# The shifted queries of a second attention layer: one VectorE subtraction from PSUM becomes a ScalarE copy and a GpSimd subtraction

## The chip, the core and the metric

The kernel runs on one core of a Trainium2 chip. The metric is the time of one execution on the device, in microseconds (us). Profile lines come from one further execution that the hardware profiler recorded; times in them count from the start of its span. PE is TensorE's matmul, PEld its weight load, DVE is VectorE, ACT is ScalarE, POOL is GpSimd and SP is SyncE. L12 is line 12 of the kernel.

## The reference

The program is a two-layer block of four batches of 512 tokens, 256 wide, in fp32. Each layer adds a gated cross-attention (16 heads of 16) and a gated feed-forward to the running x, each on a layer norm of x. Cut to what matters here:

```python
# layer 0: attention with biases and a decay over |t - s|, then a feed-forward with ternary weights
# layer 1:
def _L1_xattn_ref(q, k, v, Wq, Wk, Wv):
    qp = jax.nn.relu(jnp.einsum('bnd,od->bno', q, Wq))
    kp = jax.nn.relu(jnp.einsum('bnd,od->bno', k, Wk))
    vp = jax.nn.relu(jnp.einsum('bnd,od->bno', v, Wv))
    ...                                  # split into 16 heads
    E = NORM * jnp.einsum('bqhd,bkhd->bhqk', qh, kh)
    A = jax.nn.softmax(E, axis=-1)
    out = jnp.einsum('bhqk,bkhd->bqhd', A, vh)
    return out.reshape(B, N, -1)

x = x + tanh(g_xattn[0]) * _L0_xattn_ref(_layernorm(x), ctx, ctx, ...)
x = x + tanh(g_ffn[0])   * _L0_ffn_ref(_layernorm(x), ...)
x = x + tanh(g_xattn[1]) * _L1_xattn_ref(_layernorm(x), ctx, ctx, ...)
x = x + tanh(g_ffn[1])   * _L1_ffn_ref(_layernorm(x), ...)   # one of four experts for each token
```

The softmax needs each query row's largest score subtracted ahead of the exponential.

## The kernel before

**Groups and units.** The attention of both layers is cut into 32 groups, numbered in order of layer, batch, half of the features (tt) and parity of the head (e): groups 0 to 15 are layer 0, 16 to 31 layer 1, four to each batch. A group has four heads, each in 32 rows of the 128 partitions. Every group has four units, one for each 128 keys or queries, so there are 128 units; the unit u belongs to group u // 4.

**The score passes.** `scores(u, ...)` runs two kinds of score in quads. `maxima` makes scores of 128 queries against all keys for the unit six ahead (tiles pm), and VectorE reduces each 128 x 512 bank to a column of row maxima (L512). `weights` makes scores of 128 keys against all the *shifted* queries of unit u (tiles psc), and ScalarE takes the exponential of each bank (L527). A quad is two pm banks and two psc banks: that many matmuls run beside each other, since each uses 32 rows of the array. All PSUM tiles come from one ring of eight banks, so a bank that is drained late holds up the matmul that is eight allocations behind.

**The shift.** Row maxima come out with queries in the partitions, but queries stand with features in the partitions. `shifted(s)` turns the maxima tile m by four PE transposes into one bank pmT (L569), and VectorE subtracts it from the group's queries, q2 = q - pmT (L571). A spare row of each head's 32 carries the maximum, so the subtraction puts the shift into the operand of the second score pass.

**After the scores.** `weighted(s)` multiplies the exponentials with the values (L555, tile po), and ScalarE copies the result out (L561). `divided(s)` turns it by four transposes (tile pn), and VectorE takes reciprocals (L609), multiplies them with the gate in layer 1 (L611) and multiplies the weighted values with them (L616, tile o). In layer 1 it then adds o to x (L623): on GpSimd, but on VectorE for the last group of batches 2 and 3.

**The order.** Every engine executes in the order in which the program issues. After the scores of a unit, `slot(u)` issues what else belongs there. At the second of each group's units this is

```python
if u % NT == 2 and u > 0:
    s = u // NT
    if s + 1 < len(groups):
        shifted(s + 1)
        used += 0.5
    if s > 0 and not by_blocks(s - 1):
        divided(s - 1)
        used += 0.5
```

so shifted(s + 1) stands ahead of divided(s - 1), and one whole unit of scores lies between it and the first use of its q2. Behind these two, a small planner fills the slot from chains of jobs with costs and due times: layer norms (DVE statistics, POOL and ACT), projections of keys, queries and values (L455, L467, L469, L489, L491, L437, L439), the first layer's feed-forward (L668, L676, L383), the routing of tokens to experts (L755 to L772) and the dispatch lists (L816 to L1014), and the first expert tiles (L1037 and L1053 fetch rows and weights by POOL, L1090 multiplies, L1095 copies out). After the attention the remaining expert tiles follow in a hand-written queue, from about 700 us to the end.

**Tiles by tag.** A pool gives tiles with the same tag the same place. The tag "wo0" has one place of 128 x 512 fp32; it holds the first layer's output weights, which `residual` (L383) reads last for batch 3 of layer 0.

Of the kernel before, what the change touches and what calls it, by code (L numbers as in the profile page):

```python
# [11 lines left out]
F32 = mybir.dt.float32  # L12
U32 = mybir.dt.uint32
AF = mybir.ActivationFunctionType
ALU = mybir.AluOpType
# [4 lines left out]
P = 128  # L20
B, S, D = 4, 512, 256
# [30 lines left out]
def flamingo_kernel(ctx: ExitStack, tc: tile.TileContext, t: dict, out: bass.AP):  # L52
    nc = tc.nc
# [4 lines left out]
    const = ctx.enter_context(tc.tile_pool(name="const", bufs=1))  # L58
# [5 lines left out]
    def bank_psum(name):  # L64
        return ps.tile([P, 512], F32, tag="bank", name=name)
# [37 lines left out]
    wo0 = const.tile([P, NC, D], F32, tag="wo0", name="wo0")  # L103
# [288 lines left out]
    xTs, qs, ks, q2s, pos, os_ = {}, {}, {}, {}, {}, {}  # L392
# [170 lines left out]
    def shifted(s):  # L563

        g = groups[s]
        m = m_sb[g[0]][g[3]]
        pm = bank_psum(f"pmT{s}")
        for n in range(NT):
            nc.tensor.transpose(pm[:, ts(n, P)], m[:, n].rearrange("p h w -> p (h w)"), ident)  # L569
        q2s[g] = act.tile([P, S], F32, tag="q2", name=f"q2_{s}")  # L570
        nc.vector.tensor_tensor(q2s[g], qs[g], pm, ALU.subtract)  # L571

# [624 lines left out]
    def slot(u):  # L1199
# [4 lines left out]
# [8 lines that stand above are left out]
# [38 lines left out]
    for u in range(-NT, n_units):  # L1250
        if u == 0:
            shifted(0)
            early_values()
            other_constants()
        if u == 4:
            maxima_places(1)
        if u == first_unit(0, B - 1) + 1:
            attn_w.append(load_attn(1))
        if u == first_unit(1, 2) + 2:

            wo1 = [const.tile([P, NF // 2, D], F32, tag=f"cT{i}", name=f"wo1{i}") for i in range(2)]
            for i, w in enumerate(wo1):
                rw = t["wo1"][i * FF // 2 : (i + 1) * FF // 2, :]
                nc.sync.dma_start(out=w, in_=rw.rearrange("(c p) f -> p c f", p=P))
        vs = [u + NT] if u < 0 else [2 * u + NT, 2 * u + NT + 1] if u < LEAD - NT else [u + LEAD]
        scores(u, [v for v in vs if v < n_units])
        if u < -NT + 2:
            values[u + NT][0]()
        if u == -NT + 1:
            early_rows()  # L1270
        if u == -1:
            keys[0](halves=[1])
        if u in totals:
            job, i = totals[u]
            job(i)
        slot(u)
# [193 lines left out]
```

## Time and profile before

| What | us |
|---|---|
| median of 3 runs | 847.55 (846.2 to 848.15) |
| the profiled execution | 847.92 |
| its span | 845.8 |
| PE busy | 811.0 (96%) |
| DVE busy | 569.1 (67%) |
| ACT busy | 422.2 (50%) |
| POOL busy | 270.9 (32%) |
| DVE L571, 32 in all | 21.6 |

The span is the time from the first to the last instruction of the profiled execution. Busy shares are averages over the whole span; PE's busy time includes matmuls that wait within the array, and the ends of matmuls are modelled. In the rows of groups, the numbers behind the bar are busy time and the mean length of one in ns, and behind the second bar the idle time of the engine ahead of them with what ended it. In the timeline a row has start, length, engine, line, operation and count, and in brackets the idle time ahead of it.

### The profile page before, as it was taken

The numbers are of one execution on the slowest core, as the hardware profiler recorded it, in microseconds if no ns is written. First come the engines' busy times: TensorE is split into PE (matmuls) and PEld (weight loads), VectorE is DVE, ScalarE is ACT, GpSimd is POOL, SyncE is SP. The second block draws the span as 40 slices with busy tenths as digits, with TensorE's granted clock in tenths as the row PEclk, the third lists the DMA queues.
The fourth block names the chain that finished last, engine by engine and source line by source line (L and its number), as shares of the span: only waits on it lengthen the run. The fifth ranks groups of instructions, "written<-read, shape, count | busy, mean of one in ns | idle before, by whom it ended". The sixth has DMA issues, their size and how long they took to land. (4 is left out here: it accounts for less than half of the span.)

```text
span 845.8 us, 13576 instructions
## 1 busy us (share of the span) xinstructions
PE 811.0 (96%) x5220; PEld 452.4 (53%) x5220; DVE 569.1 (67%) x1272; ACT 422.2 (50%) x884; POOL 270.9 (32%) x439
## 2 busy tenths in 40 slices
PE   6999999999999999999999999999999999898994
PEld 3444444535464345544474444554545557787993
DVE  6768868766857776568737676558688654786443
ACT  2475555653645453455426474346556667332341
POOL 5536445524333243321101120002103314526522
PEclk9999999999999999999999999999999999999997
DMA  8200000000001000000000010000104422707730
GB/s 314 68 1 1 1 1 1 2 1 1 1 1 38 1 1 1 1 26 1 1 1 26 1 46 6 1 1 1 51 2 150 144 96 89 255 13 243 258 138 19
DMA packets 17712, 42.27 MB, mean 50 GB/s; under 512 B 2033, under 2 KB 12017, under 8 KB 15217
## 3 DMA queue, kind: packets, MB, share of 16 engines
q0 software_dynamic: 5104, 27.34, 9.3%
q1 hardware_dynamic: 12128, 13.54, 4.7%
q8 instruction: 41, 0.67, 0.3%
q10 hardware_dynamic: 416, 0.54, 0.2%
q14 instruction: 23, 0.18, 0.1%
HBM read 35.13 MB, written 6.29 MB: 49 GB/s over the span
## 5 line engine op out<-in xcount | busy, mean ns | idle before, releaser
L512 DVE TENSOR_REDUCE m<-pm 128x1 f32<-128x512 f32 x512 | 316.7, 681 | 109.0 <-PE psc L498 106.5
L527 ACT ACTIVATE p<-psc 128x512 f32<-128x512 f32 x512 | 267.1, 602 | 151.8 <-PE psc L498 149.4
L498 PE MATMUL psc<-q,k 32*128 32x512 f32 x1024 | 278.7, 623 | 0.2 <-DVE h L676 0.2
L498 PE MATMUL pm<-k,q 32*128 32x512 f32 x1024 | 262.7, 616 | 1.5 <-ACT q L485 0.9
L530 POOL TENSOR_TENSOR p<-p,dec 128x256 f32<-128x256 f32 x128 | 93.7, 736 | 178.7 <-ACT p L527 178.7
L498 PEld LDWEIGHTS pm<-k,q 32*128 32x128 f32 x1024 | 92.9, 184 | 84.1 <-issue 50.2
L498 PEld LDWEIGHTS psc<-q,k 32*128 32x128 f32 x1024 | 106.3, 184 | 52.0 <-issue 25.9
L555 PE MATMUL po<-p,v 128*32 128x512 f32 x1024 | 116.5, 595 | 1.9 <-DVE m L512 1.9
L555 PEld LDWEIGHTS po<-p,v 128*32 128x32 f32 x1024 | 31.7, 109 | 81.8 <-issue 60.8
L1090 PE MATMUL pg<-xs,wg 128*128 128x128 f32 x608 | 71.6, 276 | 0.4 <-DVE m L512 0.4
L1090 PEld LDWEIGHTS pg<-xs,wg 128*128 128x128 f32 x608 | 69.8, 192 | 3.8 <-DVE m L512 1.4
L623 POOL TENSOR_TENSOR x<-x,o 128x256 f32<-128x256 f32 x14 | 10.2, 727 | 174.4 <-DVE o L616 131.7
L1116 ACT ACTIVATE ha<-pg,wg 128x128 f32<-128x128 f32 x120 | 34.2, 368 | 53.0 <-PE pg L1090 53.0
L668 PE MATMUL ph<-xTf,w1q 128*128 128x512 f32 x128 | 60.0, 605 | 0.0
L1285 PE MATMUL pyf<-wo,ha 128*128 128x256 f32 x256 | 59.3, 387 | 0.0
L383 PE MATMUL py_f<-w2q,h 128*128 128x256 f32 x256 | 57.2, 381 | 0.0
L561 ACT COPY oT<-po 128x512 f32<-128x512 f32 x32 | 18.7, 584 | 77.1 <-PE po L555 77.1
L383 PEld LDWEIGHTS py_f<-w2q,h 128*128 128x128 f32 x256 | 48.0, 190 | 9.3 <-DVE m L512 3.0
L1285 PEld LDWEIGHTS pyf<-wo,ha 128*128 128x128 f32 x256 | 48.7, 195 | 6.4
L455 PE MATMUL pk<-cT,wk 128*128 128x512 f32 x68 | 35.3, 644 | 7.2 <-DMA cT<-in_ctxT_dram 7.2
L668 PEld LDWEIGHTS ph<-xTf,w1q 128*128 128x128 f32 x128 | 22.6, 189 | 30.4 <-issue 18.2
L388 DVE SCALAR_TENSOR_TENSOR x<-py_f,tg,x 128x512 f32<-128x512 f32 x8 | 6.0, 751 | 42.8 <-PE py_f L383 42.8
(256 smaller groups left out, 816.5 us busy)
## 6 DMA issues: line engine op xcount, KB each, us to landing
x<-in_x_dram SPq DMA_DIRECT2D x4, 512.0 KB, 8.7
rows_d<-xn_f SPq DMA_DIRECT2D x4, 512.0 KB, 3.0
rows_d<-x SPq DMA_DIRECT2D x4, 512.0 KB, 3.4
cT<-in_ctxT_dram SPq DMA_DIRECT2D x3, 512.0 KB, 9.5
w1q<-in_w_dram SPq DMA_DIRECT2D x1, 1024.0 KB, 9.0
w2q<-in_w_dram SPq DMA_DIRECT2D x1, 1024.0 KB, 11.3
wo<-in_wo_dram SPq DMA_DIRECT2D x2, 512.0 KB, 3.8
rows<-in_rows_dram SPq DMA_DIRECT2D x1, 640.0 KB, 9.2
```

The costliest lines, as they stand in the source:

```text
L383: nc.tensor.matmul(py[:, n, :], lhsT=operand(c, n0 + n), rhs=w[:, c, :], start=(c == 0), stop=(c == chunks - 1),)
L455: nc.tensor.matmul(pp, lhsT=attn_w[layer][w][:, c, ts(tt, P)], rhs=src[:, c, :], start=(c == 0), stop=(c == NC - 1),)
L498: nc.tensor.matmul(out_, lhsT=lhs[r, ts(n, P)], rhs=rhs[r, :], start=True, stop=True)
L512: nc.vector.tensor_reduce(m[:, n, 2 * pair + i, r : r + 1], pm[i], AX.X, ALU.max)
L527: nc.scalar.activation(p[:, i, :], psc[i], AF.Exp, scale=SCALE)
L530: nc.gpsimd.tensor_tensor(d, d, dec.unsqueeze(1).to_broadcast([P, 2, P]), ALU.mult)
L555: nc.tensor.matmul(po[i * HP : (i + 1) * HP, :], lhsT=v_sb[b % 2][0][:, kt, c0 : c0 + HP], rhs=ps_exp[NT * s + kt, i // 2][:, i % 2, :], s ...
L561: nc.scalar.copy(pos[s], po)
L668: nc.tensor.matmul(ph, lhsT=w1q[:, c, ts(f, P)], rhs=st["xT"][:, c, :], start=(c == 0), stop=(c == NC - 1),)
L1090: nc.tensor.matmul(ph[:, f, :], lhsT=w[:, c, ts(f2 * NF // 2 + f, P)], rhs=xs[j][:, c, :], start=(c == 0), stop=(c == NC - 1),)
L1116: nc.scalar.activation(ha[:, f, :], (ha if src is None else src)[:, f, :], AF.Gelu, bias=biases[j][:, fa : fa + 1],)
L1285: nc.tensor.matmul(py, lhsT=hs[j, f // 4][:, f % 4, :], rhs=wo1[f // 4][:, f % 4, :], start=(f == 0), stop=(f == NF - 1),)
```

## The change

For the groups of layer 1 from batch 1 on (groups 20 to 31, twelve calls), `shifted` no longer lets VectorE subtract from PSUM. ScalarE copies the bank pmT into a tile in SBUF, whose place is that of wo0, and GpSimd subtracts this tile from the queries. The other twenty groups are as before, and so is the order in which things are issued.

```diff
@@ -568,7 +568,13 @@
         for n in range(NT):
             nc.tensor.transpose(pm[:, ts(n, P)], m[:, n].rearrange("p h w -> p (h w)"), ident)
         q2s[g] = act.tile([P, S], F32, tag="q2", name=f"q2_{s}")
-        nc.vector.tensor_tensor(q2s[g], qs[g], pm, ALU.subtract)
+        if g[0] == 1 and g[1] > 0:
+
+            turned = const.tile([P, S], F32, tag="wo0", name=f"mT{s}")
+            nc.scalar.copy(turned, pm)
+            nc.gpsimd.tensor_tensor(q2s[g], qs[g], turned, ALU.subtract)
+        else:
+            nc.vector.tensor_tensor(q2s[g], qs[g], pm, ALU.subtract)
```

## The prediction

> **What bounds the kernel now.** I read the page first, then the busy time by stage, then the rows of the instructions that the change touches, and last the timeline around each of the twelve places where it acts. The twelve lie between 456.6 and 684.3 us (layer 1, batches 1 to 3), so that stage is what counts.
>
> ```profile
> 455.00:700.00 245.00, 242.11 (x1669) 122.06 (x1666) 169.42 (x376) 137.20 (x266) 42.25 (x74) 1.00 0.13 45
> ```
>
> The columns are the window, its length, then busy time of PE, PEld, DVE, ACT and POOL, clock, DMA. TensorE has a matmul in flight for 242.1 of 245.0 us at full clock. VectorE is busy 69%, ScalarE 56%, GpSimd 17%. So there are only 2.9 us in which PE stands quite still, and time can be won only there and where PE runs one of its two score streams (pm, psc) alone because a PSUM bank is not free yet.
>
> ```profile
> L571 DVE TENSOR_TENSOR q<-q,pmT 128x512 f32<-128x512 f32 x32 | 21.6, 675 | 1.1 <-PE pmT L569 1.1
> ...
> L561 ACT COPY oT<-po 128x512 f32<-128x512 f32 x32 | 18.7, 584 | 77.1 <-PE po L555 77.1
> ...
> L623 POOL TENSOR_TENSOR x<-x,o 128x256 f32<-128x256 f32 x14 | 10.2, 727 | 174.4 <-DVE o L616 131.7 <-DVE top L755 31.9 <-DVE left_d L816 10.8
> ...
> L725 POOL TENSOR_TENSOR x<-x,rows 128x1024 f32<-128x1024 f32 x3 | 7.1, 2358 | 6.3 <-ACT xn_f L360 6.3
> ```
>
> The first row is what is removed twelve times. The second is the price of the new ScalarE copy (same shape, also from PSUM). The last two bracket the new GpSimd subtraction.
>
> Now one of the twelve places, group 25, in order of time (start, length, engine):
>
> ```profile
> 569.48 0.66 PE L569 MATMUL pmT<-ident,m 128*128 128x128 f32 x4
> ...
> 570.67 0.67 DVE L571 TENSOR_TENSOR q<-q,pmT 128x512 f32<-128x512 f32 x1
> ...
> 571.26 0.25 DVE L609 RECIPROCAL rec<-pn 128x16 f32<-128x16 f32 x1
> ...
> 571.80 2.31 ACT L527 ACTIVATE p<-psc 128x512 f32<-128x512 f32 x4 [1.10 <-PE psc L498]
> ...
> 571.81 0.42 DVE L616 TENSOR_TENSOR o<-pn,rec 128x256 f32<-128x256 f32 x1
> ...
> 572.31 0.73 POOL L623 TENSOR_TENSOR x<-x,o 128x256 f32<-128x256 f32 x1 [23.19 <-DVE o L616]
> ...
> 573.23 2.45 DVE L512 TENSOR_REDUCE m<-pm 128x1 f32<-128x512 f32 x4
> ...
> 573.95 0.30 PEld L498 LDWEIGHTS pm<-k,q 32*128 32x128 f32 x4 [1.30 <-DVE m L512]
> ...
> 577.39 3.64 PE L555 MATMUL po<-p,v 128*32 128x512 f32 x32 [0.52 <-DVE m L512]
> ```
>
> VectorE runs without a pause from L571 to the reductions, and twice PE waits for a reduction to free a bank. ScalarE stands idle 1.10 us just after the transposes, and GpSimd has been idle 23 us. Here the moved 0.675 us is on the path.
>
> **The change part by part.** Of 32 shifted() calls, 20 keep L571. For the other twelve:
>
> 1. *Removed from DVE*: each L571 holds DVE from its start to the next instruction's start, 0.60 us (570.67 to 571.26 above; starts overlap). I use 0.60, 12 x 0.60 = 7.2 us of DVE work.
>
> 2. *Added to ACT*: 12 x 0.584 = 7.0 us. From the timeline, the time between the last exponential before the transposes' end and ScalarE's next instruction is over 1 us at eleven of the twelve (group 25: 570.70 to 571.80; group 22: 498.60 to 500.15) and 0.55 us at group 30, where a small copy (lT, L747) slips by under 0.1 us with PE busy. What hides it is PE, which is still making the next scores; without that cover it would cost up to 7.0 us. The copy also frees pmT's bank, at most 0.4 us after the old subtraction's end (0.6 at group 31), and much earlier at group 28.
>
> 3. *Added to POOL*: between 728 ns for 256 elements and 2358 for 1024 a straight line gives 728 + 1630/3 = 1.27 us for 512, so 15.3 us on an engine that is idle 83%. It issues no DMA itself, but it stands ahead of L623 and of whatever that slot issues: L623 comes up to 1.0 us later, and at groups 30 and 31 so do a bias copy (L1080) and a row fetch (L1037, at 668.04 and 686.75). The trace names nobody who waited for L623, and the two fetches bring tiles 0 and 1 back for output_tile, which runs after the attention: zero, with over 10 us of cover. SP's queue is not touched.
>
> 4. *The longer way to q2*: the copy starts when ACT's last exponential ends, takes 0.58, POOL starts 0.14 us after ACT (median of 54 such hand-overs from L527 to L530), 1.27 more: about 2.0 us. Before, it was DVE's backlog plus 0.67. The first score that reads q2 comes 3.2 us or more after the old subtraction's end at eleven groups and 2.27 us after it at group 28 (632.39 to 634.67). The new way ends 0.8 to 2.0 us later than the old one, but at group 28 about 0.9 us *earlier* (ACT is free at 629.47, DVE only at 631.72). Priced at zero, cover at least 1.8 us (group 25); each us beyond that would be lost whole, PE having nothing else to do. The single turned buffer is rewritten four units (some 20 us) later, and its place (wo0) was last read by layer 0: also zero.
>
> 5. *What DVE's 0.60 us is worth*, place by place:
>  - group 25: two PE waits on L512, as shown. -0.60.
>  - group 28: the second score quad's psc starts at 633.34, right after L616 frees pn's bank at 633.29. -0.50, less than the whole because an earlier pm of that quad is limited otherwise.
>  - groups 23 and 27: a score waits for DVE's L676 (PE stands 0.18 us, PEld 1.01) and L439 (PEld 0.67). In both, DVE's route chain sits before it, see below. -0.40 and -0.50.
>  - group 21: PE's next job waits 0.11 us beyond the usual 0.76. -0.10.
>  - groups 20, 22, 26: DVE idles 0.5 to 0.7 us a little later, waiting for ScalarE's half of the same bank (L437, L467), which waits for PE. 0.
>  - groups 24, 30, 31: DVE idles 2.4 to 5.3 us right behind, or PE is busy with output products. 0.
>  - group 29: next paragraph. +0.50.
>
> **The port.** The row that speaks against the change is this, at group 27 (and likewise at 521.52, and L820 at 685.28, 0.79 us):
>
> ```profile
> 611.16 0.73 POOL L623 TENSOR_TENSOR x<-x,o 128x256 f32<-128x256 f32 x1 [15.96 <-DVE top L755]
> ...
> 611.41 0.52 DVE L758 TENSOR_TENSOR onehot<-onehot,order 128x16 f32<-128x16 f32 x1
> ```
>
> and the group of that instruction (minimum, median, maximum in ns):
>
> ```profile
> L758 DVE TENSOR_TENSOR onehot<-onehot,order x4: 174/345/515, 521.5 to 732.9; 128x16 f32<-128x16 f32 x4
> ```
>
> L758 takes 174 ns alone and 515 ns when a GpSimd tensor_tensor runs; it ends 0.03 us after that does. [...] At groups 23 and 27, L758 would now arrive at about 520.9 and 610.75 and be let in when the subtraction ends (521.4, 611.35), still 0.5 to 0.6 us before its old end; hence the gains above. At group 29, the last addition of batch 2 runs on DVE with two SBUF inputs (L623, 648.29 to 648.71). It would arrive at 647.65, meet a subtraction of 647.6 to 648.9 and end at 649.25: 0.5 us late, with bn_stats and four reductions queued behind it, and PE's L1090 waiting for the first of those already. Hence +0.50.
>
> [...]
>
> Sum: -0.60 - 0.50 - 0.40 - 0.50 - 0.10 + 0.50 = -1.6 us. The profiled execution took 847.92 us (span 845.8 and 2.1 around it), so its counterpart is 846.3; the median of the runs is 847.55, 0.37 lower, which makes 845.9. The tail after 700 us begins with work handed down from this stage, so I carry the shift through unchanged.
>
> **The rivals.**
> - *DVE limits more than the gaps show* (0.17). VectorE's four reductions need 2.4 us of a bare unit of 2.5 us, and PE's modelled ends hide waits. If nine of twelve places pass on the whole 0.60, the gain is 5.4 - 0.5 = about 4.9 us: 842.6. Against it: the 2.9 us of standing PE in the stage.
> - *PE is the bound and gives nothing* (0.13). Each early release is met by a later wait for PE or ACT (DVE idles on psc 39.5 us in this stage). 847.5.
> [...]
> - *The edit acts late*, with q2 waited for by PE: needs 1.8 us and more beyond the worked-out way; I fold it into the slower case.
>
> **How the numbers follow.** The likeliest case has 0.45: its own range is -3.0 to 0, centred on 1.6, and about 0.2% (1.7 us) is also what a measurement of this kernel can tell from no change, so it splits into 0.25 faster and 0.20 same. Faster: 0.25 + 0.17 = 0.42; same: 0.20 + 0.13 = 0.33; slower: 0.25. The range 843.2 to 849.6 leaves out most of the strong gain's upper half and the port's full price, together about 0.2.
>
> **What would show it.** L571 x20; twelve L561-like copies of about 0.58 us from PSUM; POOL subtractions of 1.2 to 1.35 us; L611 at 234 ns in all (right) or above 1 us in some (the port); DVE's L623 at group 29 stretched from 424 ns to over 1 us; the 1.30 us wait at group 25 back near 0.7; no PE wait that names POOL's q2. A PE wait on q2, ACT's exponentials starting later behind the copy, or subtractions over 2 us would make the prediction wrong.

## The result, and the profile after

| | before | after |
|---|---|---|
| median of 18 runs (us) | 846.92 | 845.87 |
| range (us) | 846.16 to 848.25 | 844.03 to 846.76 |
| profiled execution, span (us) | 847.92, 845.8 | 846.76, 845.1 |

The ratio is 0.9982, 95% interval 0.9975 to 0.9989: 1.5 us less by the ratio, between 0.9 and 2.1. By the medians it is 1.05 us, because this before, over 18 runs, lies 0.6 us under the three runs that the forecast started from. The forecast was -1.65 us, which lies within this interval.

The stage of the change, in the same window as before (PE, PEld, DVE, ACT, POOL, clock, DMA):

```profile
455.00:700.00 245.00, 242.07 (x1684) 123.15 (x1678) 167.35 (x366) 144.34 (x281) 58.30 (x86) 1.00 0.13 45
```

VectorE is busy 2.1 us less, ScalarE 7.1 us more, GpSimd 16.1 us more, and PE is as busy as before. VectorE should have lost 7.2 us by the removed instructions alone. Some 3 us of that came back as instructions that were held, most of it in the L617 row and the last row of the groups below. The work also runs earlier by then, so that the last 2 us of the window hold 0.7 us that lay behind it before. The rest, over 1 us, is not accounted for.

```profile
L575 POOL TENSOR_TENSOR q<-q,mT 128x512 f32<-128x512 f32 x12 | 15.3, 1272 | 131.3 <-ACT mT L574 131.3
L577 DVE TENSOR_TENSOR q<-q,pmT 128x512 f32<-128x512 f32 x20 | 13.5, 676 | 0.0
...
L629 POOL TENSOR_TENSOR x<-x,o 128x256 f32<-128x256 f32 x14 | 10.2, 727 | 32.6 <-DVE o L622 32.6
...
L574 ACT COPY mT<-pmT 128x512 f32<-128x512 f32 x12 | 7.2, 601 | 0.1
...
L617 DVE TENSOR_SCALAR rec<-rec,tg 128x16 f32<-128x16 f32 x16 | 5.7, 355 | 0.6
...
L629 DVE TENSOR_TENSOR x<-x,o 128x256 f32<-128x256 f32 x2 | 1.6, 808 | 0.1
```

(The multiplication by the gate, L611 before, is L617 here; the addition of o to x, L623, is L629; the product o, L616, is L622; lines behind shift by six.) The copy and the subtraction cost about what was forecast. The mean of L617 has gone from 234 to 355 ns and that of VectorE's own L629 from 424 to 808.

Group 25 again, a few rows of the timeline (its transposes come behind unit 98, which is the third unit of group 24, not the second):

```profile
570.30 0.59 ACT L574 COPY mT<-pmT 128x512 f32<-128x512 f32 x1
...
570.38 0.25 DVE L615 RECIPROCAL rec<-pn 128x16 f32<-128x16 f32 x1
...
570.66 0.23 DVE L617 TENSOR_SCALAR rec<-rec,tg 128x16 f32<-128x16 f32 x1
...
570.97 1.27 POOL L575 TENSOR_TENSOR q<-q,mT 128x512 f32<-128x512 f32 x1 [21.73 <-ACT mT L574]
...
571.46 2.21 ACT L527 ACTIVATE p<-psc 128x512 f32<-128x512 f32 x4 [0.56 <-PE psc L498]
...
572.35 2.45 DVE L512 TENSOR_REDUCE m<-pm 128x1 f32<-128x512 f32 x4
573.06 0.30 PEld L498 LDWEIGHTS pm<-k,q 32*128 32x128 f32 x4 [1.30 <-DVE m L512]
...
576.51 1.07 PE L555 MATMUL po<-p,v 128*32 128x512 f32 x8 [0.52 <-DVE m L512]
```

PE's two waits on L512 are still 1.30 and 0.52 us long; the prediction's sign, that the first would come down to about 0.7, is not there. It was a wrong sign, not a missing gain: from the transposes (569.19) to po (576.51) it is now 7.32 us, before 7.91 (569.48 to 577.39). PE came to both waits as late as VectorE let it, in both kernels.

So a list of waits cannot show where the gain lies; the start of each unit's scores can. Measured against group 20's transposes (which removes a common shift of 0.21 us at the start of the two recordings), the first psc matmul of each unit moves only at these places:

| place | forecast (us) | after - before (us) |
|---|---|---|
| group 20 | 0 | +0.09, taken back one unit later |
| group 21 | -0.10 | -0.10 |
| group 23 | -0.40 | -0.47, +0.07 |
| group 25 | -0.60 | -0.50, -0.09 |
| group 27 | -0.50 | -0.46 |
| group 28 | -0.50 | -0.42, -0.09 |
| group 29 | +0.50 | +0.26 |
| 22, 24, 26, 30, 31 | 0 | 0 |
| sum | -1.60 | -1.80 |

The +0.07 of group 23 comes at unit 95. It stands there too in a kernel below that leaves group 23 as it was, so it cannot be put down to that group's subtraction.

At unit 127, the last, a further -0.27 stands: in unit 126 before, PE waits that much for an exponential. It stands in every kernel below that has ScalarE's copy anywhere, also in one that leaves group 31 as it was, and not in the one without any copy. Why is not settled, and I leave it out of the sums.

### The profile page after: what moved, and what is told of

Its sections match the earlier page's. It is cut to its first block, busy times and chain, and to the rows that moved or that the text cites. A ratio compares the mean times of both kernels' runs of the same rounds, so it can differ in the third digit from the quotient of the medians.

```text
span 845.1 us, 13599 instructions
## 1 busy us (share of the span) xinstructions
PE 809.8 (96%) x5220; PEld 453.4 (54%) x5220; DVE 566.5 (67%) x1260; ACT 428.4 (51%) x896; POOL 286.7 (34%) x451
## 5 line engine op out<-in xcount | busy, mean ns | idle before, releaser
L512 DVE TENSOR_REDUCE m<-pm 128x1 f32<-128x512 f32 x512 | 317.0, 682 | 109.6 <-PE psc L498 107.0
L575 POOL TENSOR_TENSOR q<-q,mT 128x512 f32<-128x512 f32 x12 | 15.3, 1272 | 131.3 <-ACT mT L574 131.3
```

What stands on the lines that cost most here:

```text
L512: nc.vector.tensor_reduce(m[:, n, 2 * pair + i, r : r + 1], pm[i], AX.X, ALU.max)
```

## The experiments

In all of them "step at a unit" is the reading of the table above: how far the unit's first psc matmul moves against the recording of before, less what the unit ahead of it had moved. There is one recording of each kernel. Ratios are against the kernel before on the same chip.

**Five of the twelve.** The theory: a saved VectorE instruction is worth something only where PE is waiting for VectorE.

```diff
-        if g[0] == 1 and g[1] > 0:
+        if s in (21, 23, 25, 27, 28):
```

> The ScalarE copy and GpSimd subtraction at groups 21, 23, 25, 27 and 28 alone; the other seven go back to VectorE's subtraction from PSUM. Measured by where PE stands: start of a unit's scores against the same unit of the kernel before, from group 20's transposes on. Theory (VectorE's 0.6 us is worth something only where PE waits for VectorE): all of the gain stays, -2.1 us at the end of the attention (-0.10, -0.46, -0.58, -0.46, -0.52), without the +0.26 at group 29 and without a -0.28 seen at the last unit: median about 845.8. Rival (each of the twelve places gives its share): 5/12 of 2.07, -0.9 us.

Measured: -0.10, -0.47 and +0.07, -0.51 and -0.08, -0.46, -0.42 and -0.09: every step of the change within 0.01 us, -2.06 by unit 113. In the recorded execution PE then loses 1.8 us at units 114 and 115, of which 0.25 comes back at unit 116; the next run comes back to this. The timed runs: 846.66 against 848.58 us, ratio 0.9978 (0.9968 to 0.9987), -1.9 us. The five carry the whole gain; a share for each of twelve (-0.9) lies outside the interval only just, but the steps leave no room for it.

**The other seven.**

```diff
-        if g[0] == 1 and g[1] > 0:
+        if s in (20, 22, 24, 26, 29, 30, 31):
```

> The complement: groups 20, 22, 24, 26, 29, 30 and 31 alone. Theory: nothing at 20, 22, 24, 26 and 30, about +0.26 at group 29 where VectorE's two-input addition of o to x stands behind the subtraction, -0.28 at the last unit; in sum 0. The multiplication by the gate lasts 1.2 us at groups 20 and 24 again. Rival (each place gives its share): 7/12 of 2.07, -1.2 us.

Measured in a single execution (854.12 us, which alone is no time to compare): up to unit 113 there is +0.09 and -0.09 at group 20, +0.07 at unit 95 and +0.06 at unit 111, in sum +0.13 us where the rival wanted some -0.7 by then (four shares). L617 lasts 1.17 us at group 20 and 1.24 at group 24, as in the change. Units 114 and 115 then take 4.9 us longer and group 29 cannot be read. Of that, about 3.4 us is the clock by estimate (half of a stretch of 6.8 us):

```profile
640.00:655.00 15.00, 14.72 (x82) 8.72 (x78) 8.37 (x17) 6.42 (x13) 4.89 (x6) 0.77 0.51 192
```

In these 15 us the granted clock is 0.77 (before: 1.00): it is halved from 646.4 to 653.2 us. The rest, some 1.5 us, is about the loss that the five show too, at the same units and at a granted clock of 1.00; there ScalarE and VectorE wait 1.6 and 0.7 us for scores. Of the four kernels that ran on this chip (the five, the seven and the next two) three lose 1.8 us or nearly that much here and the fourth 0.3; the change loses nothing, nor do the last four kernels, which ran on another chip. The kernel before takes 848.58 us on this chip and 846.71 on the other, so it may have the loss here as well, but there is no recording of that. The loss falls together with the first indirect fetches of expert weights (L1059, issued at 635.2 and 637.8 us in the run of the five); its cause stays open.

**VectorE subtracts from ScalarE's copy.** With the change two things come earlier: VectorE is free, and at some places pmT's bank. This run keeps the copy and gives VectorE its subtraction back.

```diff
             nc.scalar.copy(turned, pm)
-            nc.gpsimd.tensor_tensor(q2s[g], qs[g], turned, ALU.subtract)
+            nc.vector.tensor_tensor(q2s[g], qs[g], turned, ALU.subtract)
```

> Half of the change at all twelve: ScalarE copies pmT out, but VectorE subtracts, from the copy. VectorE has its 0.67 us back and now waits for ScalarE too. Theory (VectorE's time is what was worth something): no gain; +0.3 to +0.7 us at groups 21, 23, 25, 27 and 29 each where the copy ends that much after VectorE was free, 0 at 28; +1 to +2.5 us in sum. Rival (the gain comes from pmT's bank being free earlier, at group 28 above all): -0.5 at group 28 stays.

Measured: 851.08 against 848.58, ratio 1.0029 (1.0015 to 1.0043), +2.5 us. The steps: +0.33 at 21, +2.02 at 23, +0.56 at 25, +0.33 at 27, +0.01 at unit 112 (group 28), +0.30 at units 114 and 115, +0.63 at 29. A halved clock for 3.4 us (525.9 to 529.3) lies within the step at 23. The routing on VectorE that this step hangs on (see the last experiments) ends 0.34 us later, which leaves 1.68 us for the clock, half of its stretch; without that the sum is +2.5, like the timed runs. One row shows what VectorE pays at group 25:

```profile
573.60 0.69 DVE L575 TENSOR_TENSOR q<-q,mT 128x512 f32<-128x512 f32 x1 [0.46 <-ACT mT L574]
```

The bank is free early here, and nothing is won; at group 28, where VectorE does not wait for the copy, the unit starts as before, and the rival's -0.5 is not there. (The 0.30 us at units 114 and 115 stand where the other kernels on this chip lose theirs, and are left open with them.) So VectorE's time was what counted. That ScalarE may copy at no cost to itself does not mean that VectorE may wait for it.

**Copy and subtraction in halves.** In the change L617 starts 0.08 us ahead of the subtraction at groups 21, 22, 23 and 27 (478.15 against 478.23 at group 21), and lasts 234 ns; at 20 and 24 it starts 0.13 and 0.07 us behind it, and lasts 1.18 and 1.22. In the change at group 20:

```profile
458.17 1.27 POOL L575 TENSOR_TENSOR q<-q,mT 128x512 f32<-128x512 f32 x1 [4.47 <-ACT mT L574]
458.30 1.18 DVE L617 TENSOR_SCALAR rec<-rec,tg 128x16 f32<-128x16 f32 x1
```

To tell whether that order is the cause, GpSimd starts earlier here. If it is, L617 lasts about 0.6 us at 21, 22, 23 and 27 too, by an estimate from half of the subtraction's 1.27 us, the gains at 21, 23 and 27 shrink by 0.3 to 0.5 us each where they have that much, and the sum goes from -2.1 to about -1.2 us. With another cause it stays at 234 ns and the sum at -2.1.

```diff
-            nc.scalar.copy(turned, pm)
-            nc.gpsimd.tensor_tensor(q2s[g], qs[g], turned, ALU.subtract)
+            for i in range(2):
+                part = ts(i, S // 2)
+                nc.scalar.copy(turned[:, part], pm[:, part])
+                nc.gpsimd.tensor_tensor(
+                    q2s[g][:, part], qs[g][:, part], turned[:, part], ALU.subtract
+                )
```

> The change with copy and subtraction in two halves of 256 columns each, so that GpSimd starts some 0.2 us earlier, ahead of the multiplication by the gate. [...]

Measured in a single execution (847.61 us): L617 (here L621) lasts 0.62 to 0.63 us at 21, 22, 23 and 27, where it was 0.234, and 0.41 and 0.47 at 20 and 24, whose subtraction is now shorter:

```profile
L621 DVE TENSOR_SCALAR rec<-rec,tg x16: 233/235/628, 405.9 to 708.3; 128x16 f32<-128x16 f32 x16
```

Steps: 23 gives -0.13 in place of -0.47, 27 -0.13 in place of -0.46; 21 keeps -0.11, since little was asked of it, and 25 and 28 are as in the change. Sum by unit 113: -1.40 against -2.06. Two misses: nothing of the 0.10 at 21 was lost, and L621 was shut out at group 29 as well (0.61 us), where I had it ahead. So the order of the two is the cause. Splitting the work for an earlier q2 makes it worse: nobody waits for q2, and VectorE meets the first half.

**The subtraction three times.** How much later may q2 come?

```diff
             nc.gpsimd.tensor_tensor(q2s[g], qs[g], turned, ALU.subtract)
+            nc.gpsimd.tensor_tensor(q2s[g], qs[g], turned, ALU.subtract)
+            nc.gpsimd.tensor_tensor(q2s[g], qs[g], turned, ALU.subtract)
```

> The change with the GpSimd subtraction issued three times in a row (the same result each time), so q2 comes 2.55 us later. Theory (the long way to q2 costs nothing since its cover is 1.5 us at group 25 and 2.7 us or more elsewhere): PE waits for GpSimd's q2 at group 25 alone, about +1.0 us at unit 100, and nowhere else; VectorE's second two-input instruction of the routing (L766) at groups 23 and 27 is let in only after the second subtraction, +0.5 to +0.7 us each; sum about -2.1 + 1.0 + 1.2 = 0. Rival (q2 was already awaited in the change and hides in PE's modelled times): 2.5 us at each of the twelve places, +20 us and more.

Measured in a single execution (847.89 us): PE waits for the third subtraction at group 25 (0.79 us of PE standing, rows below), and the unit starts 0.71 us late in place of 0.50 early; one unit later 0.92 us has come back. At group 31, whose cover of 2.7 us is nearly used up, another 0.2 us is lost; at the other ten PE does not wait.

```profile
574.25 1.26 POOL L577 TENSOR_TENSOR q<-q,mT 128x512 f32<-128x512 f32 x1
...
575.56 1.16 PE L498 MATMUL psc<-q,k 32*128 32x512 f32 x8 [0.79 <-POOL q L577]
```

Groups 23 and 27 go from a gain of 0.46 each to a loss of 0.19, as forecast, because the routing's second two-input instruction (L766 of the change) is let in only after the second subtraction: here it lasts 1.10 us, alone 0.17.

```profile
521.36 0.17 DVE L767 TENSOR_REDUCE top<-onehot 128x4 f32<-128x16 f32 x1
521.57 1.10 DVE L768 TENSOR_TENSOR onehot<-onehot,top 128x16 f32<-128x16 f32 x1
```

The sum by unit 126 is +0.6 (0 forecast). In the change the first score that reads q2 starts 1.52 us after the subtraction's end at group 25, where step 4 had at least 1.8 (it left out that PE itself comes 0.50 us earlier there), and 2.7 us or more after it elsewhere. The rival with 2.5 us at each place is far off.

**The gate without its multiplication.** If VectorE's time is what counts, any other instruction taken from the same chain must be worth the same. The ones column beside the values makes the softmax sums; with 1/gate in it, the reciprocal brings the gate along.

```diff
+                if layer == 1 and b < 2 and n0 == 0:
+                    nc.gpsimd.tensor_copy(
+                        vh[:, :, :, DK], ginv.unsqueeze(2).to_broadcast([P, NT, H])
+                    )
...
         nc.vector.reciprocal(rec, pn[:, :, :, DK])
-        if layer == 1:
-            nc.vector.tensor_scalar_mul(rec, rec, gx1)
```

(ginv is one reciprocal of the gate's column at the start.) First on the kernel before, with its subtraction on VectorE everywhere:

> [...] Theory (VectorE's time counts at the same five places and at group 29, whatever instruction it is taken from; 0.27 us each): about -0.1 at 21, -0.27 at 23, 25 and 27, -0.2 at 28, -0.18 at 29, in sum -1.2 us. Rival (it was the early bank or the earlier q2, not VectorE's time): 0.

Measured: steps of -0.10 at 21 (0.05 of it back), -0.27 each at 23, 25, 27 and 28, -0.25 at 29; sum -1.38. Timed: 845.57 against 846.71, ratio 0.9988 (0.9980 to 0.9997), -1.0 us. Sixteen instructions of 0.27 us, and again five places, with group 29 as a sixth since nothing stands in its way there, give all of it.

Then with the five groups on ScalarE and GpSimd:

> The five useful groups by ScalarE and GpSimd, and the multiplication by the gate taken out as in the run before. Theory: -2.06 from the five and a further -0.27 at 25, up to -0.2 at 23, 28 and 29, little at 21 and 27 whose waits are used up: about -2.8 us, median 844.7 against 847.5. Rival (the first saving has used up all waits): -2.1 us.

Measured: -2.62 by unit 126 where -2.8 was expected (25: -0.76 and -0.10; 29: -0.25; the others within 0.02 us of the five). Timed: 844.29 against 846.71, ratio 0.9973 (0.9961 to 0.9985), -2.3 us. This has the lowest median of the kernels; its interval overlaps that of the change, so that it beats the change rests on the steps (0.8 us), not on the ratio.

Groups 23, 27 and 28 gave almost nothing further, for two reasons. At 28, as at 21, the waits for VectorE seem used up by the first 0.60 us: VectorE now stands idle for 0.20 us ahead of a reduction there. At 23 and 27 it is the hold by GpSimd. The routing's first instruction with two SBUF inputs (L768 here, L764 of the change) arrives 0.27 us earlier, but ends only when the subtraction has ended, and so lasts 0.64 us in place of 0.37; the second one (L770, L766 of the change) then stands behind the addition of o to x:

```profile
518.84 1.27 POOL L581 TENSOR_TENSOR q<-q,mT 128x512 f32<-128x512 f32 x1 [14.66 <-ACT mT L580]
...
519.50 0.64 DVE L768 TENSOR_TENSOR onehot<-onehot,order 128x16 f32<-128x16 f32 x1
...
520.07 0.73 POOL L633 TENSOR_TENSOR x<-x,o 128x256 f32<-128x256 f32 x1
...
520.38 0.45 DVE L770 TENSOR_TENSOR onehot<-onehot,top 128x16 f32<-128x16 f32 x1
```

Behind that second instruction stands L676 of before, for which a score waits at group 23. The step there follows the end of the instruction wherever the clock was full (both against before, less the shift of the unit ahead; group 27 agrees as well, to 0.01 us):

| run | its end (us) | step at 23 (us) |
|---|---|---|
| the change | -0.46 | -0.47 |
| the five | -0.46 | -0.46 |
| halves | -0.13 | -0.13 |
| three times | +0.19 | +0.19 |
| gate taken out, before | -0.27 | -0.27 |
| gate taken out, five | -0.48 | -0.48 |

And with all twelve:

> All twelve groups by ScalarE and GpSimd, and the multiplication by the gate taken out. Theory: as with the five, but at group 29 VectorE's addition of o to x still stands behind the subtraction until it ends, which now starts as early as before, so the loss there stays or grows by the 0.27 us that are no use: about -2.4 us.

Measured: steps as with the five except +0.26 at 29 in place of -0.25; -2.12 by unit 126. Timed: 844.65 against 846.71, ratio 0.9975 (0.9967 to 0.9982), -2.1 us. At group 29, as at 23 and 27, VectorE arrives 0.27 us earlier than in the change and is held that much longer: its addition lasts 1.46 us in place of 1.19.

```profile
645.50 1.46 DVE L633 TENSOR_TENSOR x<-x,o 128x256 f32<-128x256 f32 x1
```

## Why the prediction was right

- *The view of the bound.* That PE has something in flight for 242 of 245 us, so that only the few places where a bank comes late can give anything, was right, and the place-by-place list held: the largest miss is 0.24 us, at group 29. The five and the seven show that the list is the mechanism and not a sum that happened to fit. Why group 28 gives less than the whole 0.60 us was not tested.
- *The single number.* That the median after, 845.87, falls on the forecast 845.9 is in part luck: the forecast started from a median 0.63 us higher, and the gain by the medians is 0.60 us smaller. The ratio, -1.5 us, is the fair comparison.
- *Steps 1 to 3 (costs on each engine).* VectorE's 0.60 us at a place, the copy (0.601 measured, 0.584 forecast) and the subtraction (1.272 against 1.27) held. The straight line between 256 and 1024 elements was good to 2 ns.
- *Step 4 (the longer way to q2).* Zero, and the triple shows where it would have stopped being zero, although the cover at group 25 was 1.52 us and not 1.8. One term was off: ScalarE's end to GpSimd's start is 0.08 us at most places here, not the 0.14 taken from the hand-overs of layer 0.
- *Step 5, groups 23 and 27.* Both gains came out near their terms by two misses that nearly cancel. The subtraction held the routing's first instruction with two SBUF inputs as foreseen, but let it end some 0.74 us earlier than before, not 0.5 to 0.6. The second one, which the prediction did not have, was then held by the addition of o to x (174 to 450 ns) and gave 0.28 back. The rows are of before and then of the change, at group 23:

```profile
522.27 0.17 DVE L760 TENSOR_TENSOR onehot<-onehot,top 128x16 f32<-128x16 f32 x1
```

```profile
520.09 1.28 POOL L575 TENSOR_TENSOR q<-q,mT 128x512 f32<-128x512 f32 x1 [14.66 <-ACT mT L574]
...
521.02 0.37 DVE L764 TENSOR_TENSOR onehot<-onehot,order 128x16 f32<-128x16 f32 x1
...
521.33 0.73 POOL L629 TENSOR_TENSOR x<-x,o 128x256 f32<-128x256 f32 x1
...
521.63 0.45 DVE L766 TENSOR_TENSOR onehot<-onehot,top 128x16 f32<-128x16 f32 x1
```

- *Step 5, group 29.* VectorE's addition lasted 1.19 us in place of 0.42, as foreseen, but it ended 0.25 us late (in the time of before) and not 0.54: the subtraction ended 0.2 us earlier than worked out, and the addition 0.27 us behind it and not 0.35. All of this reached PE, whose old wait of 0.18 us for a bank grew to 0.44:

```profile
645.57 1.27 POOL L575 TENSOR_TENSOR q<-q,mT 128x512 f32<-128x512 f32 x1 [3.32 <-ACT mT L574]
...
645.92 1.19 DVE L629 TENSOR_TENSOR x<-x,o 128x256 f32<-128x256 f32 x1
...
649.02 2.05 PE L1096 MATMUL pg<-xs,wg 128*128 128x128 f32 x16 [0.44 <-DVE m L512]
```

- *The port.* "The port's full price", which the range leaves out, and the chance of 0.25 for slower stand for a term that no run shows. What the runs show in its place is a hold that depends on the order: L617 takes 234 ns when it starts first, 1.18 and 1.22 us behind the subtraction at groups 20 and 24, and 0.62 to 0.63 us at 21, 22, 23 and 27 in the halves, where GpSimd is first. In the trace of before no tensor_scalar showed it: L611 takes 233 to 236 ns in all sixteen, and L155, a tensor_scalar of 128 elements for each partition, 342 to 346 ns in all four, although GpSimd's L337 ran beside it. That the sum has no term for the multiplication rested on an estimate from the rows of before, that it would start about 0.25 us ahead of the subtraction at groups 21, 22, 23 and 27. It was ahead by 0.08 us: the copy's record starts 0.14 us ahead of the end of the exponential before it, and GpSimd follows 0.06 us sooner than reckoned, while the copy itself takes 0.62 us there. With so little to spare, the zero was partly luck. In the halves, where the multiplication is held at 23 and 27, it cost 0.34 us at each.
- *"Carried through unchanged"* is the weakest step. In the recorded execution the shift is -1.80 just ahead of the last unit and -2.07 at it, and -0.96 at the end. What lies between is the clock, in the same window of 15 us, before and after:

```profile
760.00:775.00 15.00, 10.80 (x64) 9.41 (x63) 10.98 (x53) 2.52 (x9) 9.67 (x11) 0.89 0.71 238
```

```profile
760.00:775.00 15.00, 11.80 (x64) 10.51 (x65) 10.58 (x50) 3.00 (x10) 9.92 (x11) 0.77 0.80 272
```

  The granted clock there is 0.77, against 0.89 before: it is halved for 6.8 us (762.4 to 769.3) in place of 3.4, and output products that take 0.38 us at full clock take 0.63. The gate run with five loses 1.0 us behind the last unit too, at the same 0.77; the one with all twelve, at 0.89, loses nothing (-2.40 at the last unit, -2.81 at the end). So in these recordings the shift is handed through, up to some 0.4 us, except for the stretches of halved clock, whose length differs from recording to recording.

## What to carry to other kernels

A saving on an engine that is not the bound is worth its size at those places where the bound's next buffer comes out of that engine's unbroken run, and nothing elsewhere; list the places and read each one. Before moving a two-input operation to GpSimd, look at what VectorE does in the microsecond behind it: a VectorE instruction with two SBUF inputs, and a small tensor_scalar too, may be held until it ends (here 174 ns became 450, 424 became 1192 and 234 became 1224), and which of them comes first can hang on less than 0.1 us (here 0.08). Behind such a hold, time saved ahead of it is worth nothing, as at groups 23, 27 and 29. By the steps it was best here to move the work at five places of twelve and to take away the small instruction that was held behind GpSimd at groups 20 and 24.

## What the runs showed of the hardware

- A tensor_scalar of 16 fp32 elements for each partition is held by a GpSimd tensor_tensor: 234 ns alone, 1176 and 1224 ns when it comes 0.13 and 0.07 us behind it. A waiting VectorE instruction seems to get in between two GpSimd instructions in a row: L764 (in the change, 521.02 us) ends 0.02 us after the subtraction, at 521.39, although GpSimd's next one is recorded from 521.33 on.
- The granted clock drops to one half for 3.4 or 6.8 us at a time. At 28.0 us it does so in the recordings of before and of the change (0.91 over 20 to 40 us), and not in that of before with the gate taken out (1.00). Over 760 to 775 us it is 0.89 in the recordings of before, of the five, of before with the gate taken out and of all twelve with it taken out, and 0.77 in those of the change and of the five with the gate taken out. It also drops amid matmuls, at 526 us where VectorE subtracts from the copy and at 646 us with the seven, and from about 837 us to the end in before. What sets it off is open. Where VectorE subtracts from the copy, PE is busy 14.6 of 15 us around 526 us and 3.06 us of the 3.5 ahead of it:

```profile
520.00:535.00 15.00, 14.56 (x64) 9.68 (x65) 7.12 (x21) 2.44 (x5) 0.73 (x1) 0.89 0.00 0
522.40:525.90 3.50, 3.06 (x19) 1.42 (x14) 3.43 (x8) 2.17 (x4) 0.30 (x1) 1.00 0.00 0
```

  In the 18 runs of the change the mean granted clock and the time go together: 844.0 to 845.2 us in the five runs at 0.991 or 0.992, 846.0 to 846.8 in the seven at 0.989. That spread is more than the effect of the change, and it is why the steps, which repeat to 0.01 us up to unit 113, told more than the times.
